# A state-space scan with a build-time planner: eight w buffers and four quads of rows, C products given to GpSimd by its lead, the shared weights prepared in the prologue

## The chip, the cores and the metric

The kernel runs on one core of one Trainium2 chip. The metric is the time of one execution on the device in microseconds (us). Three runs of the kernel before gave 6493.72, 6498.34 and 6510.17 us; the median is 6498.34 us. About 0.3% (20 us) is what such a measurement can tell apart.

In the text the engines have the names of the profile: PE is TensorE (matmuls), PEld its weight loads, DVE is VectorE, ACT is ScalarE, POOL is GpSimd, and SP is the engine whose queue issues all DMAs of this kernel.

## The reference, cut to what matters

Four images (batches) of 96 channels by 64 x 64 positions go through four layers, all in float32. Layer 0 is a two-dimensional selective scan. This is its core:

```python
xi = silu(depthwise_conv3x3(in_proj(layernorm(x))[:192]))        # 192 channels, 4096 positions
xs = [rows, columns, rows reversed, columns reversed]            # four directions k
dt = softplus(dt_proj(x_proj(xs)));  Bs, Cs = x_proj(xs)         # 16 states n
def step(hst, inp):
    dA = exp(dt_t[..., None] * A[None])
    dBx = dt_t[..., None] * B_t[:, :, None, :] * x_t[..., None]
    hst = hst * dA + dBx
    y_t = einsum('bkdn,bkn->bkd', hst, C_t)
```

Each of 192 channels has 16 states in 4 directions, and each state runs along 4096 positions. The sum over the states gives y. Then come a norm, a gate with silu(z), an output projection and a two-layer perceptron (the "tail" in the kernel). Layer 1 is a smaller scan (two directions, one state), layer 2 a Fourier transform over the positions with a perceptron in 8-bit floats, and layer 3 a linear attention with another such perceptron.

## The kernel before, in words

**The scan loop.** The scan of layer 0 is cut into 64 steps: four batches, four directions in the order 0, 1, 3, 2, four chunks of 1024 positions. A step has 24 units, numbered j (three groups of channels), q (four groups of states, the "quads") and p (two halves); a unit is a tile of 128 rows (32 channels by 4 states) by 1024 positions. There are 1536 units. For each of them

- `sources` (line 1517): POOL multiplies w = u * bb, where u is dt * x and bb holds the rows of B, broadcast by DMA;
- `decays` (1496): ACT computes h = exp(dt * A) into PSUM, which has two buffers for h, and copies the last state of the unit two before;
- `recurs` (1528): DVE scans h and w into h (TENSOR_TENSOR_SCAN), and then multiplies w = h * cc, the "C product", where cc holds the rows of C;
- `gathers` (1566): PE adds up the four states and the quads of w into the PSUM tile py, two units at a time, and then w is free.

The C product of some units is put aside: there the scan writes into w, and POOL multiplies w = w * cc (`side`, 1557). `aside` (1492) picks every 12th unit (11, 23, 35, ...), 127 in all.

**The buffers** are counted in line 1370: `WB, DB, RB, SIDE = 6, 3, 5, 12`. There are six w buffers: source i waits until the pair that holds unit i - 6 has been summed. There are three pairs of u and dt, and five each of bb and cc, one per quad of a step: the load for a quad waits until the quad five before it has been read for the last time (`loads_bc`, 1474). The u, dt, bb and cc tiles are 512 KB each as written on chip.

**The prelude of a step** (`preludes`, 1389) loads xi (four DMAs, `load_packed`), multiplies it by xw on PE, forms dt and dt * x (two POOL products of 128 x 1536 named dtu) and stores them to DRAM (dd, bc), from where the broadcast loads above read them.

**The background.** One thread, `others` (1647), does the rest while the loop runs, in series: `prepare` (folds weights of the tail and of layers 1 to 3 and stores them to DRAM as `prep_d`), then `front(b)` of batches 1 to 3 (norm, in-projection in four jobs two at a time, depthwise convolution, xi stored by rows and by columns), and then `rest(b)` of each batch: the tail with its four gates and eight groups, layer 1, and layers 2 and 3. The tail's chunks go in the order 3, 2, 1, 0, each when the loop has stored that chunk of y; the tail of a batch ends with BATCH_NORM_AGGREGATE. Batch 0's front runs alone ahead of the loop, in the prologue; after the loop what is left of batch 3 runs alone, with more banks and with DVE in POOL's place ("wide").

Each `front(b)` loads the in-projection's weights w_raw, multiplies them by the norm's bias and gain, centres them into w_in, and loads the convolution's diagonal weights dgs (two DMAs of 576 KB) right after.

**What sets the order.** No instruction is placed by hand. At build time a planner (class `Work`) keeps a clock for every engine, with a cost in us for every instruction (a POOL product of 1024 columns 2.36, a scan 2.34, a C product 1.23, a DMA 0.45 in SP's queue, then bytes/280e3 and 2.0 to land). Each thread says with `on(engine, events...)` what it waits for. The planner advances the thread that could start first (`choose`, 162; at equal times the lower rank), and the instructions are issued in that order on each engine. An engine works its own queue in order, so an instruction whose input is later than planned holds up all behind it. `wk_.me.end += t` tells the planner that what was just done takes t longer. The prologue ends for the planner when a condition holds (1663); only then are the pools for u, dt, bb, cc, w and Y opened, and the threads of the loop started.

All elementwise calls go through one helper, so nearly all DVE and POOL rows have line L254, ACT's L242 or L231, PE's L227, loads L275 and stores L279. The names of the tiles tell them apart.

Of the kernel before, what the change touches and what calls it, by code (L numbers as in the profile page):

```python
# [216 lines left out]
def tile_hybrid(ctx: ExitStack, tc: tile.TileContext, I: dict, out: bass.AP):  # L217
# [126 lines left out]
    l1A = const.tile([128, 2], F32, name="l1A")  # L344
    dsum = const.tile([128, 4], F32, name="dsum")
    centd = const.tile([C, C], F32, name="centd")
    diagD = const.tile([128, 3, 128], F32, name="diagD")

    xi_d = [dram.tile([2, NG, DI, HC], F32, name=f"xi_d{b}") for b in range(B)]
    z_d = [dram.tile([NG, DI, HC], F32, name=f"z_d{b}") for b in range(B)]  # L350
    y_d = [dram.tile([128, 3, 2048], F32, name=f"y_d{b}") for b in range(B)]
    x1_d = [dram.tile([C, L], F32, name=f"x1_d{b}") for b in range(B)]
    PREP = 1358
    prep = dram.tile([128, PREP], F32, name="prep_d")
    y1_d = [dram.tile([C, L], F32, name=f"y1_d{b}") for b in range(B)]
# [117 lines left out]
    def front(b):  # L473
        stx, (px_,) = pools(bg("fx"))
        xp01 = px_.tile([128, 66, 66], F32, name="xp01")
        xp2 = px_.tile([128, 34, 66], F32, name="xp2")
        dgs = [px_.tile([128, 9, 128], F32, name=f"dg{i}") for i in range(2)]
        ahead_ = b == 0
        if ahead_:
            stc, (xtp, ck) = pools(bg("f2"), bg("f2w"))  # L480
            xts = [xtp.tile([128, 64, rows], F32, name=f"xt{rows}") for rows in (64, 32)]
        st, (wp, wk) = pools(bg("f1"), bg("f1w"))
        w_raw = wp.tile([C, 384], F32, name="w_raw")
        w_in = wp.tile([C, 384], F32, name="w_in")
        yield on("sp")
        get(w_raw, I["w_inT"])
        yield on("pool")
        for xp, n in ((xp01, 66), (xp2, 34)):
            po_.memset(xp[:, :, 0:1], 0.0)
# [2 lines left out]
        po_.memset(xp01[:, 65, :], 0.0)  # L492
        po_.memset(xp2[0:64, 0, :], 0.0)
        po_.memset(xp2[64:128, 33, :], 0.0)
        (pb,) = yield on("pe", banks=1)
        for col, lo, m, r in ((0, 0, 128, 0), (1, 128, 64, 0), (1, 128, 64, 64), (2, 192, 128, 0), (3, 320, 64, 0), (3, 320, 64, 64)):
            mm(pb[r : r + m, col : col + 1], lhsT=w_raw[:, lo : lo + m], rhs=V("b1", C), start=True, stop=True)
        bias = wp.tile([128, 4], F32, name="bias")
        yield on("dve")
        ve.tensor_add(bias, pb[:, 0:4], V("bi", n=4))  # L500
        ve.tensor_scalar(w_raw, w_raw, V("g1", C), None, ALU.mult)
        drop(pb)
        yield from centred(w_in, w_raw, 384)
        xv = I["x"][b].rearrange("c (h g t) -> c g h t", h=2, t=HC)

        def inproj(gp):
# [63 lines left out]

            return job

        yield on("sp")
        for i in range(2):
            get(dgs[i], I[("dg01", "dg2")[i]])

        def conv(part, q):
            dg, xt, xp = dgs[part], xts[part], (xp01, xp2)[part]
# [38 lines left out]
        order = [(0, 0), (0, 1), (1, 0), (1, 1)] if ahead_ else []  # L617
        if ahead_:
            soon = wk_.add(par([conv(p, q) for p, q in order], 2))
        yield from par([inproj(gp) for gp in range(4)], 2, 4)  # L620
        if ahead_:
            yield on(None, lambda: soon.end if soon.done else None)
        st.close()
# [2 lines left out]

        if not ahead_:
            stc, (xtp, ck) = pools(bg("f2"), bg("f2w"))
            xts = [xtp.tile([128, 64, rows], F32, name=f"xt{rows}") for rows in (64, 32)]
        rest_ = [(p, q) for q in range(2, 4) for p in (1, 0)] if ahead_ else []  # L630
        rest_ += [(p, q) for p in (1, 0) for q in range(8 - 4 * p) if (p, q) not in order + rest_]
# [639 lines left out]

    def prepare():

        st, (wp,) = pools(bg("prep"))
        o = wp.tile([128, PREP], F32, name="prep")
        m1, tbias = o[0:C, 0:384], o[:, 384:387]
        dtc = o[0 : C + 1, 387:587].rearrange("p (k c) -> p k c", k=2)
# [6 lines left out]
        sc = wp.tile([C + 1, DI], F32, name="sc")  # L1284
        var, gam = (wp.tile([C, 1, C], F32, name=n) for n in ("var", "gam"))
        wq, sc1 = (wp.tile([C, C], F32, name=n) for n in ("wq", "sc1"))
        yield on("pool")
        po_.memset(o, 0.0)
        yield on("sp")
        get(m1, I["mlp1T"])  # L1290
# [25 lines left out]
        yield on("act")  # L1316
        copy(dtc[0:C, :, 0:C], pw[0:C, 0 : 2 * C].rearrange("p (k c) -> p k c", k=2))
        drop(pw)
        wk_.me.end += 15.0
        yield on("act", took=1.5, table=LN_EXP)  # L1320
        rstd(sc, bn[:, 3, :])
        rstd(var, var)
# [44 lines left out]
    ]  # L1367
    NS_ = len(steps)
    NU = UNITS * NS_
    WB, DB, RB, SIDE = 6, 3, 5, 12  # L1370
    made, weights, summed = {}, {}, {}
    anti = mybir.DependencyInfo(mybir.DependencyClass.Sync, mybir.DependencyReason.ANTI)
    live = dict(h={}, w={}, state={}, Y=None, py=None)
    fg = {}

    def place(i):
        n = i % UNITS
# [11 lines left out]
    def preludes():  # L1389
        ck, dp = fg["ck"], fg["dp"]  # L1390
        for g, (b, k, s, c) in enumerate(steps):
            need = [("front", b)] if k % 2 else rows_of(b, c)
            if g >= 3:
                need.append(("du", 6 * (g - 3) + 5))
            if g >= 1:
                need.append(("src", unit(g - 1, 0, 0, 0)))
            yield on("sp", *need)
            if s == 0:
                xw = ck.tile([128, 3, 128], F32, tag="xw", name="xw", bufs=1)
                get(xw, I["xw"][:, k])  # L1400
                dtw = ck.tile([64, 3, 128], F32, tag="dtw", name="dtw", bufs=1)
                get(dtw, I["dtw"][:, k])
                weights[b, k] = xw, dtw
            xw, dtw = weights[b, k]
            xi = ck.tile([128, 3, HC], F32, tag="xi", name="xi", bufs=1)
            load_packed(xi, xi_d[b][k % 2], c)
            d = made[g] = {}
            (px,) = yield on("pe", banks=1)
            for j in range(3):
                mm(px, lhsT=xw[:, j, :], rhs=xi[:, j, :], start=(j == 0), stop=(j == 2))  # L1410
            xd = ck.tile([128, HC], F32, tag="xd", name="xd", bufs=1)
            yield on("act")
            act(xd, px, AF.Identity, bias=V("ones"))
            drop(px)
            yield on("sp")
            bc = dp.tile([32, 2, HC], F32, tag="bc", name="bc")
            for hf in range(2):
                put(bc[:, hf], xd[64 + 32 * hf : 96 + 32 * hf])
            d["bc"] = bc.rearrange("n f t -> n (f t)")
            post("bc", g, stored=True)  # L1420
            dtu = ck.tile([128, 2, 3, HC], F32, tag="dtu", name="dtu", bufs=1)
            dd = d["dd"] = dp.tile([2, 3, 2, 32, 2, HC], F32, tag="dd", name="dd")
            for j0, j1 in ((0, 1), (1, 2), (2, 3)) if g == 0 else ((0, 3),):
                js = slice(j0, j1)
                for j in range(j0, j1):
                    (pd,) = yield on("pe", banks=1)
                    mm(pd, lhsT=dtw[:, j, :], rhs=xd[0:64], start=True, stop=True)
                    yield on("act", took=1.3)
                    act(dtu[:, 0, j], pd, AF.Abs)
                    act(dtu[:, 1, j], pd, AF.Relu)  # L1430
                    drop(pd)
                yield on("act", took=1.6, table=LN_EXP)
                act(dtu[:, 0, js], dtu[:, 0, js], AF.Exp, scale=-1.0)
                yield on("act", took=1.6, table=LN_EXP)
                act(dtu[:, 0, js], dtu[:, 0, js], AF.Ln, bias=one)
                if g == 0 and j1 == 3:
                    post("begun")
                yield on("pool")
                po_.tensor_add(dtu[:, 0, js], dtu[:, 0, js], dtu[:, 1, js])
                yield on("pool")  # L1440
                po_.tensor_mul(dtu[:, 1, js], dtu[:, 0, js], xi[:, js])
                yield on("sp")
                for p in range(2):
                    for hf in range(2):
                        r = p * 64 + hf * 32
                        put(
                            dd[:, js, p, :, hf, :].rearrange("t j d i -> d t j i"),
                            dtu[r : r + 32, :, js],
                        )
                for j in range(j0, j1):  # L1450
                    post("dd", g, j, stored=True)
            sync()
            post("dd", g)
# [35 lines left out]
                post(tag, n)  # L1489
                wk_.detach()  # L1490

    def aside(i):

        return i % SIDE == SIDE - 1 and i < NU - 1

    def decays():
        for i in range(NU + 2):
            if i >= 2:
                yield on("act", ("scan" if aside(i - 2) else "C", i - 2), *([("dt", 6 * place(i)[0] + 2 * place(i)[1] + place(i)[3])] if i < NU else []), took=1.3, table=LN_EXP, unit=min(i, NU - 1))
                g, j, q, p, n = place(i - 2)  # L1500
                b, k, s, c = steps[g]
                h = live["h"].pop(i - 2)
# [25 lines left out]
    def recurs():  # L1528
        for i in range(NU):
# [8 lines left out]
                live["state"][b, k] = fg["ck"].tile([128, 24], F32, tag="state", name="state")  # L1538
            h, w, state = live["h"][i], live["w"][i], live["state"][b, k]
            first = 0.0 if s == 0 else state[:, n : n + 1]  # L1540
            o = w if aside(i) else h
            if k >= 2:
                it = ve.tensor_tensor_scan(o[:, ::-1], h[:, ::-1], w[:, ::-1], first, ALU.mult, ALU.add)
            else:
# [3 lines left out]
                tc.add_manual_dep(it.ins, summed.pop(i - WB), anti, reason="sums of what lay in w")  # L1548
            if o is w:
                post("scan", i)  # L1550
                live["h"][i] = o
                continue
            yield on("dve")
            ve.tensor_mul(w, h, made[g]["cc", q])
            post("C", i)

    def side():

        for i in filter(aside, range(NU)):
            g, j, q, p, n = place(i)  # L1560
            yield on("pool", ("scan", i), *([("st", i)] if steps[g][2] < NCH - 1 else []))
            w = live["w"][i]
            po_.tensor_mul(w, w, made[g]["cc", q])
            post("C", i)

    def gathers():

# [78 lines left out]

    def others():
        yield on(None, ("front", 0))
        yield from prepare()
        for b in range(1, B):  # L1650
            yield from front(b)
        for b in range(B):
# [2 lines left out]
    with tc.manual_schedule():  # L1655
# [3 lines left out]
        st_ck, (ck, dp) = pools(sb("ck", 2), dict(name="sd", bufs=3, space=DRAM))  # L1659
        fg.update(ck=ck, dp=dp)  # L1660
        first = wk_.add(setup()), wk_.add(front(0))
        ts = [wk_.add(preludes(), 0)]
        wk_.run(
            lambda: first[0].done and ("inproj", 0) in wk_.events
            and not any(k.startswith("bs") for k in wk_.held.values())
        )
        mode["wide"] = False
# [193 lines left out]
```

## Time and profile before

| | us |
|---|---|
| median of three runs (6493.72 to 6510.17) | 6498.34 |
| the profiled execution | 6480.99 |
| its span, first to last instruction | 6479.2 |
| first scan of the loop starts | 92.1 |
| last C product of the loop ends | 5936.9 |
| DVE busy in the span | 5790.4 (89%) |
| PE busy | 5160.7 (80%) |
| POOL busy | 4737.6 (73%) |
| ACT busy | 4306.2 (66%) |

A group of the profile is a line, an engine, an operation and the tiles written and read, then the shape and the count; after the bar stand the busy time in us and the mean of one in ns, and after a second bar the idle time of the engine just before these instructions, with what ended most of it. In the windows view each engine has its busy us and, in brackets, its number of instructions. In the order of time a row starts with its start in us and its duration. This is the page's view of the span in 40 slices (a slice is 162 us), which shows how the loop fills DVE to slice 36 and how the rest follows:

```profile
DVE  6899999999989999999989999999989999997714
...
POOL 4778787887798787878798777787798778883000
```

The main marks of the background, from the order of time: fronts 1 to 3 begin at 277, 607 and 962 with the load of w_raw, and the third is done at 1311. The tail of batch 0 begins at 1313, those of batches 1 to 3 at 2805, 4277 and 5745, each behind the last output of the batch before (2799, 4271, 5738). Chunk 0 of y of batches 0 to 2 is stored at 1540, 3003 and 4476.

### The profile page before, as it was taken

Reading aid. Unit: us, or ns where it says so; the run is one execution under the profiler, and the core shown is the slowest. Engines: PE = TensorE matmul, PEld = TensorE weight load, DVE = VectorE, ACT = ScalarE, POOL = GpSimd, SP = SyncE. Lnnn points to the kernel's source line nnn. Section 1 sums busy time; section 2 is a strip of 40 time slices with the busy share of each in tenths; the row PEclk is TensorE's granted clock in tenths of the full one; section 3 lists DMA queues with packets and bytes.
Section 4 is the critical chain, followed back from the end, with each engine's and each line's share of the span. In section 5 each row is a group of like instructions: output and inputs, shape, how many; then the busy total and the mean of one; then the engine's idle time right before and its main releaser. Section 6 shows DMA issues by size and latency. Waiting matters only on the chain. (4 is left out here: it accounts for less than half of the span.)

```text
span 6479.2 us, 54904 instructions
## 1 busy us (share of the span) xinstructions
PE 5160.7 (80%) x15680; PEld 1622.7 (25%) x15680; DVE 5790.4 (89%) x3909; ACT 4306.2 (66%) x6506; POOL 4737.6 (73%) x2151
## 2 busy tenths in 40 slices
PE   8588887977867988767867988768868888777678
PEld 2122221222211332212211332212211332212264
DVE  6899999999989999999989999999989999997714
ACT  5465766666766558877766567877766557875635
POOL 4778787887798787878798777787798778883000
PEclk9789998988878999889979999888878999888788
DMA  5656556575565784665565785556565685552551
GB/s 170 198 186 200 172 172 192 173 221 178 161 199 173 231 274 152 187 190 181 169 197 163 226 272 172 171 184 184 179 186 166 219 283 182 166 176 82 158 153 46
DMA packets 532504, 1189.17 MB, mean 184 GB/s; under 512 B 90286, under 2 KB 163579, under 8 KB 532188
## 3 DMA queue, kind: packets, MB, share of 16 engines
q1 hardware_dynamic: 532200, 1185.66, 59.1%
q8 instruction: 124, 2.03, 0.1%
q14 instruction: 180, 1.47, 0.1%
HBM read 937.80 MB, written 247.63 MB: 183 GB/s over the span
## 5 line engine op out<-in xcount | busy, mean ns | idle before, releaser
L254 POOL TENSOR_TENSOR w<-u,bb 128x1024 f32<-128x1024 f32 x1536 | 3610.0, 2375 | 822.0 <-PE py L227 712.3
L254 DVE TENSOR_TENSOR_SCAN h<-h,state,w 128x1024 f32<-128x1024 f32 x1057 | 2483.1, 2349 | 178.5 <-ACT h L242 110.9
L227 PE MATMUL py<-w,sel 128*32 128x512 f32 x6144 | 1774.1, 937 | 424.4 <-DVE w L254 273.9
L242 ACT ACTIVATE h<-dt,negA 128x1024 f32<-128x1024 f32 x1536 | 1730.2, 1127 | 400.8 <-DVE w L254 311.0
L254 DVE TENSOR_TENSOR w<-h,cc 128x1024 f32<-128x1024 f32 x1409 | 1722.6, 1223 | 40.4
L254 DVE TENSOR_TENSOR_SCAN h<-h,w 128x1024 f32<-128x1024 f32 x352 | 805.5, 2288 | 77.6 <-ACT h L242 24.3
L231 ACT COPY state<-h 128x1 f32<-128x1 f32 x1056 | 166.0, 157 | 701.0 <-DVE w L254 699.6
L227 PEld LDWEIGHTS py<-w,sel 128*32 128x32 f32 x6144 | 182.2, 114 | 1438.6 <-DVE w L254 771.3
L254 POOL TENSOR_TENSOR w<-w,cc 128x1024 f32<-128x1024 f32 x127 | 299.1, 2355 | 114.4 <-ACT state L231 86.6
L227 PE MATMUL bm<-xp,dg 128*128 128x512 f32 x774 | 362.1, 610 | 0.0
L227 PE MATMUL bm<-xi,xw 128*128 128x512 f32 x378 | 224.6, 741 | 109.3 <-DMA xi<-xi_d 100.6
L254 POOL TENSOR_TENSOR dtu<-dtu 128x1536 f32<-128x1536 f32 (+1 forms) x66 | 221.7, 3359 | 102.3 <-ACT dtu L242 49.5
L242 ACT ACTIVATE dtu<-bm 128x512 f32<-128x512 f32 x382 | 210.0, 604 | 49.6 <-PE bm L227 48.3
L227 PE MATMUL bm<-xd,dtw 64*128 64x512 f32 x382 | 220.6, 658 | 22.8 <-ACT xd L242 9.1
L254 DVE TENSOR_TENSOR_SCAN w<-h,state,w 128x1024 f32<-128x1024 f32 x95 | 222.5, 2342 | 7.8 <-ACT h L242 4.0
L254 POOL TENSOR_TENSOR dtu<-dtu,xi 128x1536 f32<-128x1536 f32 (+1 forms) x66 | 221.2, 3352 | 4.2
L227 PEld LDWEIGHTS bm<-xp,dg 128*128 128x128 f32 x774 | 142.4, 192 | 281.3 <-issue 274.7
L227 PE MATMUL bm<-big,dg 96*96 96x512 f32 x450 | 206.0, 600 | 6.1 <-ACT state L231 4.8
L227 PE MATMUL py<-Y,eye 128*128 128x512 f32 x288 | 164.5, 654 | 53.5 <-ACT Y L231 44.3
L227 PE MATMUL bm<-x,cent 96*96 96x512 f32 x276 | 158.9, 672 | 42.8 <-POOL x L254 12.2
L242 ACT ACTIVATE bm<-bm,eps 96x512 f32<-96x512 f32 (+1 forms) x212 | 137.4, 648 | 80.1 <-PE bm L227 79.9
L242 ACT ACT_TABLE_LOAD x124 | 159.1, 1283 | 10.7 <-PE bm L227 6.9
(328 smaller groups left out, 6879.3 us busy)
## 6 DMA issues: line engine op xcount, KB each, us to landing
u<-dd SPq DMA_DIRECT2D x384, 512.0 KB
dt<-dd SPq DMA_DIRECT2D x384, 512.0 KB
bb<-bc SPq DMA_DIRECT2D x256, 512.0 KB
cc<-bc SPq DMA_DIRECT2D x256, 512.0 KB
dd<-dtu SPq DMA_DIRECT2D x252, 384.0 KB
xi<-xi_d SPq DMA_DIRECT2D x256, 192.0 KB
f_d<-fo SPq DMA_DIRECT2D x64, 384.0 KB
a<-f_d SPq DMA_DIRECT2D x64, 384.0 KB
```

Source lines behind the costliest of these rows:

```text
L227: return nc.tensor.matmul(o, lhsT=lhsT, rhs=rhs, **kw)
L231: return nc.scalar.copy(o, i, **kw)
L242: return nc.scalar.activation(o, i, func, **kw)
L254: return f(o, *a, **kw)
```

## The change

The diff, cut to its core:

```diff
+    bias = const.tile([128, 4], F32, name="bias")
+    w_d = dram.tile([C, 384], F32, name="w_d")
...
@@ front(b)
-        dgs = [px_.tile([128, 9, 128], F32, name=f"dg{i}") for i in range(2)]
         ahead_ = b == 0
         if ahead_:
+            dgs = [px_.tile([128, 9, 128], F32, name=f"dg{i}") for i in range(2)]
...
-        yield on("sp")
-        get(w_raw, I["w_inT"])
+        if not ahead_:
+            yield on("sp", ("w_in",))
+            get(w_in, w_d)
+        else:
+            w_raw = wp.tile([C, 384], F32, name="w_raw")
+            yield on("sp")
+            get(w_raw, I["w_inT"])
...
+        if ahead_:
             (pb,) = yield on("pe", banks=1)
...
             yield from centred(w_in, w_raw, 384)
+            def keep():
+                yield on("sp", ("xp", b, 3))
+                put(w_d, w_in)
+                post("w_in", stored=True)
+            wk_.add(keep())
...
-        yield from par([inproj(gp) for gp in range(4)], 2, 4)
+        yield from par([inproj(gp) for gp in range(4)], 3, 4)
...
         if not ahead_:
             stc, (xtp, ck) = pools(bg("f2"), bg("f2w"))
+            dgs = [xtp.tile([128, 9, 128], F32, name=f"dg{i}") for i in range(2)]
+            yield from taps_in()
@@ prepare()
-        st, (wp,) = pools(bg("prep"))
+        st, (wp,) = pools(sb("prep"))
...
-        yield on("pool")
+        yield on("pool", ("xp", 0, 0))
         po_.memset(o, 0.0)
...
-        wk_.me.end += 15.0
         yield on("act", took=1.5, table=LN_EXP)
@@ the loop
-    WB, DB, RB, SIDE = 6, 3, 5, 12
+    WB, DB, RB, APART, AHEAD = 8, 3, 4, 6, 4
+    sides = []
@@ preludes()
             load_packed(xi, xi_d[b][k % 2], c)
+            wk_.me.end += 2.0
@@ decays()
-                yield on("act", ("scan" if aside(i - 2) else "C", i - 2), ...
+                yield on("act", ("free", i - 2), ...
@@ recurs()
-            o = w if aside(i) else h
+            apart = i % 2 and (not sides or i - sides[-1] >= APART)
+            o = w if apart and i + AHEAD < NU and ("src", i + AHEAD) in wk_.events else h
...
             if o is w:
                 post("scan", i)
+                post("free", i)
                 live["h"][i] = o
+                sides.append(i)
                 continue
             yield on("dve")
             ve.tensor_mul(w, h, made[g]["cc", q])
             post("C", i)
+            post("free", i)
+        sides.append(None)
@@ others()
-        yield from prepare()
@@ the prologue
+        early_ = wk_.add(prepare(), 2)
         ts = [wk_.add(preludes(), 0)]
         wk_.run(
-            lambda: first[0].done and ("inproj", 0) in wk_.events
+            lambda: first[0].done and early_.done and ("inproj", 0) in wk_.events
```

What it does, part by part:

- **Which units are put aside.** The fixed list goes. When the planner reaches the scan of an odd unit i, it puts the unit aside if the last one put aside lies at least 6 units back and if the source product of unit i + 4 has already been planned. `side` follows that list as it grows: it waits for the scan, and, except in the last chunk of a direction, for ACT's copy of the state.
- **Buffers.** Eight w buffers for six, and four quads of bb and cc for five. In memory the two cancel out (two tiles of 4 KB a row each way).
- **The plan's count of an xi load** is 2.0 us longer, so that the xw matmuls are planned later.
- **prepare** leaves the background. It runs in the prologue as a thread of rank 2, from the first in-projected rows on, and the prologue isn't over for the planner before it is done. Its tiles lie where the loop's buffers are opened later. The 15 us that the plan added in its middle are gone.
- **The fronts of batches 1 to 3** load the finished w_in, which batch 0's front has stored, in place of making it again; the bias stays on chip. They load dgs only after the in-projection, into the space of the later pool, and do three in-projection jobs at a time.

The fetched weights, the products and the sums computed are the same as before.

More of the change, by code (lines that the diff above doesn't have):

```diff
@@ L482, in front @@
         st, (wp, wk) = pools(bg("f1"), bg("f1w"))
-        w_raw = wp.tile([C, 384], F32, name="w_raw")
         w_in = wp.tile([C, 384], F32, name="w_in")
-        yield on("sp")
-        get(w_raw, I["w_inT"])
+        if not ahead_:
[5 more added lines that the diff above has]
+            get(w_raw, I["w_inT"])
         yield on("pool")
@@ L494, in front @@
         po_.memset(xp2[64:128, 33, :], 0.0)
[L495 to L503, printed above, removed]
+        if ahead_:
+            (pb,) = yield on("pe", banks=1)
+            for col, lo, m, r in ((0, 0, 128, 0), (1, 128, 64, 0), (1, 128, 64, 64), (2, 192, 128, 0), (3, 320, 64, 0), (3, 320, 64, 64)):
+                mm(pb[r : r + m, col : col + 1], lhsT=w_raw[:, lo : lo + m], rhs=V("b1", C), start=True, stop=True)
+            yield on("dve")
+            ve.tensor_add(bias, pb[:, 0:4], V("bi", n=4))
+            ve.tensor_scalar(w_raw, w_raw, V("g1", C), None, ALU.mult)
+            drop(pb)
+            yield from centred(w_in, w_raw, 384)
+            def keep():
[3 more added lines that the diff above has]
+            wk_.add(keep())
         xv = I["x"][b].rearrange("c (h g t) -> c g h t", h=2, t=HC)
@@ L571, in inproj, with taps_in @@
             return job
-        yield on("sp")
-        for i in range(2):
-            get(dgs[i], I[("dg01", "dg2")[i]])
+        def taps_in():
+            yield on("sp")
+            for i in range(2):
+                get(dgs[i], I[("dg01", "dg2")[i]])
+        if ahead_:
+            yield from taps_in()
         def conv(part, q):
@@ L628, in front @@
             stc, (xtp, ck) = pools(bg("f2"), bg("f2w"))
+            dgs = [xtp.tile([128, 9, 128], F32, name=f"dg{i}") for i in range(2)]
+            yield from taps_in()
             xts = [xtp.tile([128, 64, rows], F32, name=f"xt{rows}") for rows in (64, 32)]
@@ L1490, in loads_bc @@
                 wk_.detach()
-    def aside(i):
-        return i % SIDE == SIDE - 1 and i < NU - 1
     def decays():
@@ L1498, in decays @@
             if i >= 2:
-                yield on("act", ("scan" if aside(i - 2) else "C", i - 2), *([("dt", 6 * place(i)[0] + 2 * place(i)[1] + place(i)[3])] if i < NU else []), took=1.3, table=LN_EXP, unit=min(i, NU - 1))
+                yield on("act", ("free", i - 2), *([("dt", 6 * place(i)[0] + 2 * place(i)[1] + place(i)[3])] if i < NU else []), took=1.3, table=LN_EXP, unit=min(i, NU - 1))
                 g, j, q, p, n = place(i - 2)
@@ L1555, in recurs, with chosen @@
             post("C", i)
+            post("free", i)
+        sides.append(None)
     def side():
-        for i in filter(aside, range(NU)):
-            g, j, q, p, n = place(i)
-            yield on("pool", ("scan", i), *([("st", i)] if steps[g][2] < NCH - 1 else []))
+        n = 0
+        while True:
+            def chosen():
+                if len(sides) <= n or sides[n] is None:
+                    return 0.0 if len(sides) > n else None
+                i = sides[n]
+                if steps[place(i)[0]][2] < NCH - 1:
+                    return wk_.events.get(("st", i))
+                return wk_.events["scan", i]
+            yield on("pool", chosen)
+            i = sides[n]
+            if i is None:
+                return
+            g, j, q, p, _ = place(i)
             w = live["w"][i]
@@ L1564, in side @@
             post("C", i)
+            n += 1
     def gathers():
```

## The prediction

> **What bounds the kernel now.** I read the page first, for each engine's share and for where it changes. The scan over the 1536 units of layer 0 runs on VectorE from 92.1 us to 5936.9 us, which is 90% of the span, so the answer is sought in that stretch.
>
> ```profile
> 92.00:5936.00 5844.00, 4679.95 (x14018) 1372.72 (x14019) 5526.38 (x3462) 3981.48 (x5938) 4725.64 (x2127) 0.89 0.62 191
> ```
> This is the windows view of the stretch: length, then PE, PEld, DVE, ACT and POOL busy. DVE is busy 5526 of 5844 us, which leaves 318 idle; POOL has 1118 idle. The groups view says what fills both engines.
>
> ```profile
> L254 DVE TENSOR_TENSOR w<-h,cc 128x1024 f32<-128x1024 f32 x1409 | 1722.6, 1223 | 40.4
> L254 POOL TENSOR_TENSOR w<-w,cc 128x1024 f32<-128x1024 f32 x127 | 299.1, 2355 | 114.4 <-ACT state L231 86.6
> L254 POOL TENSOR_TENSOR w<-u,bb 128x1024 f32<-128x1024 f32 x1536 | 3610.0, 2375 | 822.0 <-PE py L227 712.3
> ```
> A C product costs DVE 1223 ns, or POOL 2355 ns plus 0.90 us of wait (114.4/127). POOL's largest idle time is 712 us of waiting until PE has summed an old w. Then the waits, of DVE over the loop and of PE from 250 to 5880 us (us in total, times, longest):
>
> ```profile
> DVE h L254 <- ACT h L242: 135.3, 126, 8.3
> DVE h L254 <- ACT state L231: 57.7, 43, 8.5
> DVE h L254 <- POOL w L254: 40.1, 37, 2.6
> ```
> ```profile
> PE bm L227 <- DMA xi<-xi_d: 93.7, 31, 8.5
> ```
> DVE seldom waits for POOL. So DVE's own work sets the loop. But there is a second chain that nearly sets it too: the background thread, which does fronts 1 to 3 and then, batch by batch, tail, layer 1, 2 and 3. The order of time (start, length), SP's queue around 5738 us and then DVE at the end of batch 3's tail:
>
> ```profile
> 5671.50 0.53 SPq L279 DMA_DIRECT2D y_d<-Y  x1
> ...
> 5738.15 0.32 SPq L279 DMA_DIRECT2D out<-x  x1
> ...
> 5744.93 0.54 SPq L275 DMA_DIRECT2D rt<-in_r_tail  x1
> ```
> ```profile
> 5991.09 0.37 DVE L254 BATCH_NORM_AGGREGATE mv<-stat 96x2 f32<-96x48 f32 x1
> ```
> Chunk 3 of batch 3 was stored at 5672, but its tail began only at 5745, when batch 2's last output had gone out at 5738. The four tails end (BATCH_NORM_AGGREGATE) at 1639, 3104, 4576 and 5991: rounds of 1465 and 1472 us, against 1461 us for a batch of the loop. The two are almost equal, and a shorter loop is only worth what the background follows.
>
> **The change, part by part.**
> *More C products on POOL.* Now every 12th unit is aside (127). After it, an odd unit is aside if 6 or more have passed and POOL's source product is planned 4 units ahead. At most 1536/6, less the end, is 255. By the order of time, POOL had begun 4 units ahead at 114 of 768 odd units and 2 or more ahead at 585 (76%); with two more w buffers, a lead that the buffers cap moves up by up to two. A step's dtu products (2 x 3.4 us) and each extra aside eat that lead. Bounds: 0 and 128 extra; I take 103 (230 in all, the nearest to 76% with some delay): 103 x 1.223 = 126 us off DVE. POOL can hold it: busy 4726, waits other than for PE 406, plus 103 x 3.26 = 335, makes 5467 of some 5740.
> A table in the Trainium skill (GPSIMD Engine Reference, 4.1 Engine selection) speaks against this: two-input elementwise work belongs on VectorE, GpSimd being about twice as slow. The rows agree (2355 against 1223, 1.93 times). By that rule the products would stay and the 126 us would be nothing; the engine with 1118 us idle decides for the move.
> *POOL later for DVE.* DVE's waits for POOL are 43.8 us with 127 asides, 0.34 each: 103 x 0.34 = 36 us back. Bounds: minus 44 (eight buffers remove them all) and 103 x 2.355 = 243 (each aside holds up the next scan in full).
> *Four quads for five.* A bb or cc load may start one quad later. Between the end of the last reader and the first use, with four, today's times leave 19.7 us (median; least 14.3) for bb and 22 to 25 for cc (least 18.7). In the prologue a u load took 4.3 us from issue to use. Bounds: 0, and 63 steps x 2.2 us (73/34, a wait for u) = 136 on POOL. I take 5, since no wait for bb or cc shows in the loop's long waits.
> *Weights in the prologue.* prepare's DVE operations at 218 to 265 us sum to 12.9 us (four take about 2.3 us each), and the fronts' two on w_raw and bias to 4.5: 17 us leave the loop. Its 15 loads and the store move ahead of the first dd, u and dt loads in SP's queue; SP is idle from 12 to 44 us, then mostly waits for conv outputs, and prepare waits for the first in-projection (about 42). Some 3.5 us of DVE work falls among the depthwise taps that lead to the first scan. The loop opens only when prepare is done, and its first buffers take prepare's space. Bounds for the first scan: minus 2 and plus 20 (a chain from 42 with its 679 KB store ending at 100 instead of 80). I take plus 5. Against that, DVE's third early stall (8.3 us at 233, ACT waiting 9.8 us for a dt load queued behind those 15 loads) shrinks: minus 5.
> A rule of the Trainium skill (SBUF — State Buffer, Who interferes with whom) says that a VectorE instruction with two SBUF inputs waits for a GpSimd one that reads SBUF. The trace agrees: prepare's 96x1 products take 2274 ns beside POOL and 156 without. The C products read h from PSUM and show no such thing (1156 to 1266 ns), so more of POOL costs them nothing.
> *xi counted 2 us longer.* It moves the xw matmuls behind other PE work. Up to the 94 us of PE idle, none of it DVE's; bounds for the time 0 and minus 25 a round. *Three in-projections at once, dgs loaded late:* only in the fronts, which end at 1313 where y of batch 0 ends at 1540: 0, at worst 10 us on a front and hidden.
> Loop: -126 - 17 + 36 + 5 + 5 - 5 = **-102**, so VectorE's last product at about 5835.
>
> **What the background lets through.** Tail 0 waits for y at 1540, a quarter along, so it ends 26 us earlier. In the next two rounds chunk 1's groups end 11 us before chunk 0's gate product (3030 to 3041, 4503 to 4514): 11 us spare in each, so the last output of batch 2 comes 26 + 11 + 11 = 48 us earlier, at 5690. Tail 3 starts at 5697; its four pairs of groups took 91 and 62 us in the loop and 43 to 45 after it: 5792, 5850, 5895, 5939, against 5991. That is 52 us. PE stalls for xi returned to the background give some 6 us in each of three rounds: **70 us** in all, less than the loop's 102. From 5991 to the end (488 us) nothing changes. Own time 6481 (span 6479.2 and 1.8 around it) - 70 = 6411. The median of the runs, 6498.34, lies 17 above that execution: I predict 6428.
>
> **Rivals.** *The whole loop gain arrives* (18%): the background's steps also wait for DVE and get faster as DVE empties. For: DVE is 93% busy while layer 1 runs beside the loop (1367 of 1470 us in three windows). Against: two rounds of nearly equal length. 6498 - 102 = 6396; with all 128 asides and no added wait near 6350.
> *Nothing much* (13%): asides are hardly chosen, or POOL's lateness returns the 126 us (103 x 1.2 us a piece). 6478 to 6518.
> *Slower* (12%): the background becomes longer, through POOL. A batch's background has 84 products on POOL (64 of layer 1, 16 sums, 4 gates) in about three parallel jobs, 28 in series. Each that meets an added aside waits up to 3.26 us: 91 us a round, 274 in all, +200. It decides from 0.83 us a product (70/3/28). Against: added asides occupy 335/5740 = 6% of POOL, on average 0.1 us. For: in-order queues cluster. A midway 1.35 us a product: +44, 6542.
> My forecast has 57% (6405 to 6478). Three runs can hardly tell less than 0.3%, about 20 us, from no change: faster 0.57 + 0.18, same 0.13, slower 0.12. The range 6365 to 6500 holds the forecast, most of the first rival and about half of the second: 0.8.
>
> **What would show it.** About 230 POOL rows w<-w,cc and 1306 DVE rows w<-h,cc; POOL's wait for PE below 400 us; DVE's last product near 5835; prepare's rows before 92 and the first scan at 92 to 102; batch 2's last output near 5690, and tail 3 still starting right behind it. Rounds under 1450 would speak for the first rival, over 1475 for the last. Under 170 asides, or DVE waits for POOL above 150 us, and the step on asides is wrong. Waits for bb or cc would show that four quads are too few.

## The result, and the profile after

The changed kernel took 6386.00 us (median of five runs, 6379.59 to 6390.87) against 6498.34 (five runs, 6481.92 to 6510.17): a ratio of 0.9826, interval 0.9807 to 0.9846, or 112 us less. The profiled execution took 6390.87 us where that of before took 6480.99: 90 us less. The two differ because the profile of before lies 17 us below its median and that of after 5 us above; steps are compared between the two profiles, verdicts between the medians.

The windows view of the loop, from the first scan at 98.4 us to the last C product, which ends at 5848.8 (length, then PE, PEld, DVE, ACT and POOL busy):

```profile
98.00:5849.00 5751.00, 4669.05 (x13943) 1378.91 (x13945) 5442.87 (x3380) 3983.83 (x5935) 4873.00 (x2188) 0.88 0.61 194
```

The loop is 94 us shorter (5750 against 5845), and begins 6 us later. DVE is busy 84 us less and idle 308 us, 10 us less than before; POOL is busy 147 us more. The groups:

```profile
L254 DVE TENSOR_TENSOR w<-h,cc 128x1024 f32<-128x1024 f32 x1345 | 1644.6, 1223 | 48.1 <-DMA cc<-bc 9.4
...
L254 POOL TENSOR_TENSOR w<-w,cc 128x1024 f32<-128x1024 f32 x191 | 450.6, 2359 | 144.4 <-ACT state L231 96.9
...
L254 POOL TENSOR_TENSOR w<-u,bb 128x1024 f32<-128x1024 f32 x1536 | 3607.5, 2377 | 615.1 <-PE py L227 419.3
```

191 units went aside, not the 230 that I expected: 64 C products left DVE, 78 us. POOL's wait for PE fell from 712 to 419 us. The two more w buffers alone don't do this: the run fixed12 below has them, with the old 127 asides, and there the wait is 677 us. Most of the fall comes with the added asides, which fill POOL's idle time:

```profile
L254 POOL TENSOR_TENSOR w<-u,bb 128x1024 f32<-128x1024 f32 x1536 | 3605.4, 2377 | 809.1 <-PE py L227 677.4
```

What DVE waits for in the loop of the changed kernel, in the waits view (us in total, times, longest):

```profile
DVE h L254 <- ACT h L242: 164.7, 155, 10.4
DVE h L254 <- ACT state L231: 36.9, 31, 4.4
DVE h L254 <- POOL w L254: 23.9, 17, 5.3
```

The wait for POOL became less (24 against 40 us), the wait for ACT's h became more (165 against 135). The end of the background, from the order of time on SP's queue and then on DVE:

```profile
5590.23 0.54 SPq L279 DMA_DIRECT2D y_d<-Y  x1
...
5666.39 0.40 SPq L279 DMA_DIRECT2D out<-x  x1
...
5675.12 0.54 SPq L275 DMA_DIRECT2D rt<-in_r_tail  x1
```
```profile
5847.59 1.21 DVE L254 TENSOR_TENSOR w<-h,cc 128x1024 f32<-128x1024 f32 x1
...
5901.94 0.37 DVE L254 BATCH_NORM_AGGREGATE mv<-stat 96x2 f32<-96x48 f32 x1
```

Batch 2's last output comes 72 us earlier (5666), and the last tail ends 53 us after the last C product; before, 54 us after. So the end moved with the loop, all of it: 88 us at the loop's end, 89 at the tail's, 90 in the span.

### The profile page after: what moved, and what is told of

The parts are those of the page before. It is cut to its first block, busy times and chain, and to the rows that moved or that the text cites. A ratio compares the mean times of both kernels' runs of the same rounds, so it can differ in the third digit from the quotient of the medians.

```text
span 6389.1 us, 54746 instructions
## 1 busy us (share of the span) xinstructions
PE 5157.9 (81%) x15634; PEld 1634.6 (26%) x15634; DVE 5711.2 (89%) x3841; ACT 4319.8 (68%) x6521; POOL 4888.8 (77%) x2215
## 5 line engine op out<-in xcount | busy, mean ns | idle before, releaser
L254 DVE TENSOR_TENSOR_SCAN h<-h,state,w 128x1024 f32<-128x1024 f32 x1005 | 2360.9, 2349 | 162.0 <-ACT h L242 116.2
L227 PE MATMUL py<-w,sel 128*32 128x512 f32 x6144 | 1742.2, 939 | 447.2 <-DVE w L254 311.1
L242 ACT ACTIVATE h<-dt,negA 128x1024 f32<-128x1024 f32 x1536 | 1728.6, 1126 | 390.4 <-DVE w L254 321.0
L254 DVE TENSOR_TENSOR w<-h,cc 128x1024 f32<-128x1024 f32 x1345 | 1644.6, 1223 | 48.1 <-DMA cc<-bc 9.4
L254 DVE TENSOR_TENSOR_SCAN h<-h,w 128x1024 f32<-128x1024 f32 x340 | 777.9, 2288 | 79.4 <-ACT h L242 48.5
L254 POOL TENSOR_TENSOR w<-w,cc 128x1024 f32<-128x1024 f32 x191 | 450.6, 2359 | 144.4 <-ACT state L231 96.9
L227 PE MATMUL bm<-xp,dg 128*128 128x512 f32 x792 | 378.4, 620 | 10.2 <-DMA dg<-in_dg 10.1
L254 DVE TENSOR_TENSOR_SCAN w<-h,state,w 128x1024 f32<-128x1024 f32 x147 | 344.2, 2342 | 11.1 <-ACT h L242 7.6
L227 PE MATMUL bm<-xi,xw 128*128 128x512 f32 x384 | 213.9, 701 | 38.7 <-DMA xi<-xi_d 35.3
L227 PE MATMUL bm<-big,dg 96*96 96x512 f32 x450 | 221.4, 634 | 11.6 <-ACT u L242 6.3
```

What stands on the lines that cost most here:

```text
L227: return nc.tensor.matmul(o, lhsT=lhsT, rhs=rhs, **kw)
L242: return nc.scalar.activation(o, i, func, **kw)
L254: return f(o, *a, **kw)
```

## The experiments

Theory 1 says that the loop on DVE sets the time and what is behind it follows. Theory 2, which my prediction rested on, says that the background is as long as the loop and holds back part of any gain. Theory 3 says that the buffers, the weights and the count of xi do most of it, and the asides little. "Loop" and "idle" below are the loop's length and DVE's idle time in it, from the order of time of each profile. Ratios are to the kernel before.

| kernel | asides | us (median) | ratio (interval) | loop | idle |
|---|---|---|---|---|---|
| before | 127 | 6498 | 1 | 5845 | 318 |
| changed | 191 | 6386 | 0.9826 (0.9807 to 0.9846) | 5750 | 308 |
| fixed12 | 127 | 6438 | 0.9914 (0.9892 to 0.9937) | 5798 | 273 |
| none_aside | 0 | 6491 | 0.9995 (0.9985 to 1.0004) | 5865 | 213 |
| all_odd6 | 256 | 6464 | 0.9953 (0.9937 to 0.9968) | 5775 | 418 |
| ahead3 | 216 | 6453 | 0.9933 (0.9915 to 0.9952) | 5741 | 328 |
| tail_late | 190 | 6427 | 0.9896 (0.9879 to 0.9913) | 5751 | 313 |
| old_buffers | 5 | 6515 | 1.0018 (1.0007 to 1.0028) | 5871 | 228 |
| prep_back | 181 | 6434 | 0.9899 (0.9883 to 0.9916) | 5798 | 355 |
| no_xi | 192 | 6385 | 0.9821 (0.9799 to 0.9844) | 5749 | 323 |
| old_fronts | 188 | 6382 | 0.9825 (0.9802 to 0.9848) | 5734 | 308 |
| only_buffers | 127 | 6520 | 1.0031 (1.0020 to 1.0042) | 5898 | 360 |
| rb4 | 127 | 6514 | 1.0031 (1.0019 to 1.0042) | 5878 | 365 |
| only_prep | 127 | 6512 | 1.0021 (1.0008 to 1.0034) | 5874 | 356 |

**How many asides: the fixed list, none, every sixth unit.** Three edits of one line in `recurs`:

```diff
-            o = w if apart and i + AHEAD < NU and ("src", i + AHEAD) in wk_.events else h
+            o = w if i % 12 == 11 and i < NU - 1 else h       # fixed12
+            o = h                                             # none_aside
+            o = w if apart and i < NU - 1 else h              # all_odd6
```

> The changed kernel with the old fixed list of asides (units 11, 23, 35, ...: 127 in place of 191). Theory 1, the loop rules: 64 C products of 1.22 us come back to DVE, 78 us, so about 6464 us, and the last C product of the loop near 5925. Theory 2, the background holds part of the gain: what the loop loses was partly never had, so the time rises by less than the loop, by 20 to 50 us (6406 to 6436), the loop still by about 78. Theory 3, the gain comes mostly from the buffers, the weights and the xi count: the time stays within 20 us of 6386.

> The changed kernel with no unit aside: all 1536 C products on DVE. Theory 1: 191 x 1.223 = 234 us on top of 6386, about 6620, one for one. Theory 2: less than one for one near the changed kernel, then one for one: 6560 to 6600. If POOL's lateness costs DVE time (my 0.34 us for each aside), 191 x 0.34 = 65 us of it come back: about 6555.

> The changed kernel without the test of POOL's lead: every sixth unit aside, 256 in place of 191. Theory 1 with POOL still able: 65 x 1.223 = 80 us less, about 6306. Theory 2: the loop gets shorter, the time by 30 or less, 6355 to 6386. If POOL is late when its lead is not asked for, DVE waits for w grow from 24 us to over 100, and the time is 6370 to 6450.

With the fixed list the time was 6438, 52 us more; the loop got 47 us longer, not 78, so on average each of the 64 asides was worth 0.7 us of the loop and 0.8 us of the time in place of 1.22. It is an average and no more: the 64 lie in all four batches (10, 19, 16 and 19 of them), but against fixed12 the changed loop is shorter only in batches 2 and 3 (by 25 and 30 us) and 3 and 5 us longer in batches 0 and 1. The other 60 of the 112 us don't come from the choice of asides, so Theory 3 has about half. With none it was 6491, 105 us more for 191 asides: 0.55 each. DVE's idle time tells where the rest went. It rises with the asides: 213 us with none, 273 with 127 (0.48 for each), 308 with 191 (0.54 for each of the 64 more), 418 with 256 (1.70 for each of the last 65, which no lead was asked for). These are not waits for POOL in the first place. I sorted the idle time in front of every scan by how many units before it the last aside lay. In the changed kernel a scan right behind an aside waits 0.46 us on average (72 of 191 wait more than 0.3), all other scans 0.11. Of the 89 us that DVE waits right behind asides, 68 end with ACT's h and 18 with ACT's copy of the state. Behind an aside DVE goes from scan to scan, without the 1.22 us of a C product between, and ACT has that much less time for the next h. The wait for h in none_aside, and the waits for ACT and for POOL in all_odd6, fit this:

```profile
DVE h L254 <- ACT h L242: 77.4, 84, 8.7
```
```profile
DVE h L254 <- ACT h L242: 198.4, 166, 12.2
DVE h L254 <- POOL w L254: 68.5, 35, 7.0
```

There is a second loss, in DVE's busy time, but no price per aside can be read from it. DVE's busy time in the loop less the durations of its scans and C products is 189 us in none_aside, 218 in fixed12, 215 in the changed kernel and 209 in all_odd6. Most of the difference lies in four groups of small operations (gm, rl, kvacc times its mask, hs of the first piece), a few instructions in each batch: 24 us in none_aside, 45 in fixed12, 41 in the changed kernel, but 33 in all_odd6, with the most asides, and 30 in the kernel before. How long one of them takes goes by what POOL does at that moment; the last section shows one.

**A lead of three.** `AHEAD` 3 in place of 4:

```diff
-    WB, DB, RB, APART, AHEAD = 8, 3, 4, 6, 4
+    WB, DB, RB, APART, AHEAD = 8, 3, 4, 6, 3
```

> The changed kernel with a lead of three units asked for in place of four: some 20 to 40 more asides. At the mean price measured so far (1.22 us saved, 0.54 lost as DVE idle, some 0.2 in small DVE operations) they give 10 to 20 us: 6365 to 6380. At the price of the asides that no lead was asked for (1.7 us lost each): 6390 to 6420.

6453, which both prices miss. The loop was as expected, 25 asides more and its last C product at 5841.5, 7 us earlier than in the changed kernel. But the time was 67 us longer, so the loop doesn't set it here. SP's queue and DVE show what does:

```profile
5782.80 0.32 SPq L279 DMA_DIRECT2D out<-x  x1
...
5785.71 0.54 SPq L275 DMA_DIRECT2D rt<-in_r_tail  x1
```
```profile
5840.25 1.23 DVE L254 TENSOR_TENSOR w<-h,cc 128x1024 f32<-128x1024 f32 x1
...
5956.03 0.37 DVE L254 BATCH_NORM_AGGREGATE mv<-stat 96x2 f32<-96x48 f32 x1
```

Batch 2's last output is 116 us later than in the changed kernel. The tail of batch 3 starts only 56 us before the loop ends, and it ends 115 us after it, not 53. From the end of one tail to the last output of the batch, the background took 1214 and 1238 us in batches 1 and 2, against 1126 and 1154 in the changed kernel. all_odd6 is the same case (1224 and 1222; the span ends 589 us after the loop in place of 540). A background that becomes longer is what my last rival foresaw. In none_aside it took 1183 us in both batches and in fixed12 1159 and 1165, so its length doesn't simply grow with the asides; what lengthens it in these two kernels isn't shown.

**Is the background the bound in the changed kernel?** In tail_late the tails of batches 1 and 2 wait for one more chunk of y:

```diff
     def rest(b):
+        if b in (1, 2):
+            yield on(None, ("y", b, 1))
         st, (pp,) = pools(bg("post"))
```

> The changed kernel, but the tails of batches 1 and 2 begin only when chunk 1 of y is stored (2892 and 4326 us in the changed kernel's profile, in place of 2796 and 4209). Theory 2, the background is as long as the loop and has some 11 us spare a round: the delay of about 100 us is passed on, batch 2's last output comes 70 to 110 us later and the time rises by 50 to 90 us (6436 to 6476). Theory 1, the background has slack that only hides behind the wait for chunk 0: the time stays within 20 us of 6386.

6427, 41 us more, between the two. The loop did not change by a microsecond (5751). Only the first of the two waits held anything up: the tail of batch 1 began 84 us later, at 2879, while that of batch 2 began at 4349, behind the last output of batch 1 and after its chunk 1. The delay was passed on: the last output of batch 2 came 93 us later, and the tail ended 94 us after the last C product:

```profile
5759.68 0.32 SPq L279 DMA_DIRECT2D out<-x  x1
```
```profile
5848.63 1.23 DVE L254 TENSOR_TENSOR w<-h,cc 128x1024 f32<-128x1024 f32 x1
...
5943.35 0.37 DVE L254 BATCH_NORM_AGGREGATE mv<-stat 96x2 f32<-96x48 f32 x1
```

So of 93 us that the background came later the end felt 41; the other 52 were no loss. Not all of them need be waiting time that the changed kernel had to spare: batch 3's tail, from its load of rt to its end, takes 227 us in the changed kernel and 182 in tail_late, where more of it runs after the loop. The fourteen kernels fall into two groups: where batch 2's last output lies 182 us or more before the last C product, the span ends 536 to 548 us after that product, whatever the kernel; where it lies 91, 90 or 59 us before it (all_odd6, tail_late, ahead3), the span ends 589, 581 and 606 us after it. No kernel lies between 91 and 182, so where the one passes into the other is open: near 130 if each microsecond below it costs one, but the three points fit a half for each from 182 on as well. Theory 1 holds for the change as made, with 182, as to what sets the end; theory 2 takes over somewhere in the next 90 us.

**The buffers.** Six w buffers and five quads in the changed kernel; then eight and four, and four quads alone, in the kernel before:

```diff
-    WB, DB, RB, APART, AHEAD = 8, 3, 4, 6, 4
+    WB, DB, RB, APART, AHEAD = 6, 3, 5, 6, 4        # old_buffers
...
-    WB, DB, RB, SIDE = 6, 3, 5, 12
+    WB, DB, RB, SIDE = 8, 3, 4, 12                  # only_buffers
+    WB, DB, RB, SIDE = 6, 3, 4, 12                  # rb4
```

> The changed kernel with six w buffers and five quads. With a lead that never went above 4 in the kernel before, the test of 4 units is met at a sixth of the odd units, so I expect 60 to 110 asides, more waits of POOL for PE (over 550 us) and DVE idle near 300 us. If the buffers are what cuts DVE's idle time, 6450 to 6490; if only the number of asides counts at 0.8 us each, 80 asides against 191 make 6475; if neither does, within 20 of 6386.

> The kernel before with eight w buffers and four quads, and nothing else. The fixed-list run, with all parts of the change but the choice of asides, was 59 us faster than the kernel before, 44 of it DVE idle time in the loop. If the buffers did that: 6440 to 6465. If the weights, the fronts and the xi count did it: 6480 to 6505, and POOL's wait for PE falls without DVE getting anything. If four quads cost more than eight w buffers give: above 6505.

> The kernel before with four quads, six w buffers. The two buffer changes together cost the kernel before 20 us. If the fourth quad is the price: about 6520 or more, with waits for bb, cc. If it is the eight w buffers, which shift the order of the plan: within 10 of 6500.

With six buffers the planner found 5 units to put aside, not 60 to 110: in the plan a lead of four units hardly ever comes about (on the chip POOL had begun four units ahead at 206 of the 768 odd units). The time, 6515, is 24 us above that of none_aside, with an idle time near it (228 against 213). POOL then waits 1011 us for PE:

```profile
L254 POOL TENSOR_TENSOR w<-u,bb 128x1024 f32<-128x1024 f32 x1536 | 3598.0, 2366 | 1207.5 <-PE py L227 1011.2 <-DMA u<-dd 153.6 <-DVE w L254 17.4
```

In the kernel before, eight buffers with four quads cost 20 us and four quads alone 20 us: they are no gain in themselves, but the choice by lead needs them. Eight w buffers with five quads would leave 17.5 KB a row where Y takes 24, so the fifth quad is their price. rb4 shows no wait for bb or cc among its long ones, so late rows of B or C don't explain the 20 us. It has other stalls, the two longest of 18.5 and 16.5 us from scan to scan at 1014 and 1379 us, where the kernel before has none. Which order of the plan makes them I haven't traced.

**The weights.** prepare back in the background in the changed kernel, and in the prologue in the kernel before. This is the core of the diff; its memory, the start of its first memset and the 15 us of the plan go with it:

```diff
@@ prep_back: the changed kernel; only_prep: the reverse in the kernel before
     def others():
         yield on(None, ("front", 0))
+        yield from prepare()
...
-        early_ = wk_.add(prepare(), 2)
```

> The changed kernel with the shared weights prepared in the background again, behind front 0, as before the change. My sum gave this part 17 us of DVE's loop less 5 for the prologue. If that holds, 6392 to 6410, the first scan back at 92 us, and the step from 108 back in the loop's first three steps. The fixed-list run lost only 3 us of DVE busy time against the kernel before where I had counted 17; if the other small DVE operations had simply become longer beside a busier POOL, that stays so here and the time is 6395 to 6410; if the part is worth nothing it stays within 10 of 6386.

> The kernel before with the shared weights prepared in the prologue, and nothing else. Undoing this part in the changed kernel cost 48 us, most of it in the loop's first two steps. If it is a gain of its own (prepare and its 15 loads no longer stand between the loop's first dt and u loads): 6440 to 6465. If it is only a gain beside the other parts (front 1, three jobs at once, right behind): 6480 to 6505.

Back in the background it cost 48 us, four times my 12. The loop's first two steps took 115 and 105 us in place of 92 and 94, 34 us, and the largest piece is one stall. ACT, in prep_back's order of time:

```profile
206.18 1.12 ACT L242 ACTIVATE h<-dt,negA 128x1024 f32<-128x1024 f32 x1 [20.72 <-DMA dt<-dd]
```

SP's queue says why: 18 stores of front 0 are issued from 181.6 to 199.6 us and the next step's first u and dt loads behind them.

```profile
181.61 17.98 SPq L279 DMA_DIRECT2D xi_d<-xt  x18
199.63 0.63 SPq L275 DMA_DIRECT2D u<-dd  x1
200.31 0.60 SPq L275 DMA_DIRECT2D dt<-dd  x1
```

In the changed kernel three pairs of u and dt loads (178.6 to 186.7) go ahead of those 18 stores. So this stall is made by an order of the plan and not by prepare's own loads, which are issued only from 208.7 us; why the plan took that order isn't shown. And alone, in the kernel before, the move gained nothing: its first two steps were about 23 us shorter (91 and 89 against 95 and 109), but later stalls of 17.5 and 17.6 us at 904 and 1269 took it back, 14 us slower in all.

**xi and the fronts.** The changed kernel without the 2 us, and with the old `front(b)`:

```diff
             load_packed(xi, xi_d[b][k % 2], c)
-            wk_.me.end += 2.0                        # no_xi
...
-            get(w_in, w_d)                           # old_fronts
+        get(w_raw, I["w_inT"])
...
-        yield from par([inproj(gp) for gp in range(4)], 3, 4)
+        yield from par([inproj(gp) for gp in range(4)], 2, 4)
```

> The changed kernel without the 2 us that the plan adds to a load of xi. If the xi count only takes PE's idle time away, PE waits some 100 us for xi again and the time stays within 10 of 6386. If those stalls reach DVE through the state copies and the h tiles (ACT held up behind xd), DVE idle rises by 20 to 40 us: 6405 to 6425.

> The changed kernel with the fronts as they were (w_in made anew, dgs loaded early, two in-projection jobs at once). My sum gave this part 4.5 us. If that is its size: within 15 of 6386. The parts found so far leave some 30 us open (fixed list -59, of which the weights -48 and the buffers +20): if the fronts are those, 6405 to 6425.

Neither makes a difference (6385 and 6382 against 6386). PE's wait for xi, 100.6 us before and 35.3 in the changed kernel, is 76.5 without the 2 us, and the time is the same: these 41 us of PE's stall don't reach it.

## Why the prediction was right or wrong, point by point

The direction was right, and 6386 lies in the range 6365 to 6500, but not within my forecast's own stretch (6405 to 6478). It lies 10 us below the 6396 of the rival which I gave 18%, the whole loop gain arriving. That rival's reason, a background that gets faster, is seen in part: from the end of a tail to the last output it took 1126 and 1154 us in batches 1 and 2, in place of 1167 and 1163. That DVE is the cause isn't shown.

- **"A shorter loop is only worth what the background follows", 52 us of 102.** This step failed. I took the four pairs of groups of the last tail at 91, 62, 45 and 44 us as the tail's own pace. The last was not: it waits for chunk 0 of y, which the end of the loop gives. Counted from the load of rt, the pairs took 96, 62, 43 and 45 us before and 90, 62, 43 and 31 in the changed kernel, and the tail ends 53 us after the loop, where it was 54; in all eleven kernels whose batch 2 is done 182 us or more before the loop's end, it is 51 to 57. In tail_late only 41 of 93 us of delay reached the end, where I had every one count. My sum of the pairs also dropped 4 us (5792 with 62, 45 and 44 makes 5943, not 5939). The tail's end came 89 us earlier and not 70; 15 of these 19 us are the shorter tail (227 us from the load of rt, where I had 242), the other 4 its earlier start.
- **The rounds.** Batch 2's last output at 5666 (I said 5690, or 5672 with the 18 us that I added for PE's stalls) was near, but by luck. I had the tails of batches 0 to 2 end 26, 37 and 48 us earlier; they ended 37, 24 and 63 earlier. The rounds took 1478 and 1432 us, one beyond my sign for the last rival and one beyond that for the first, and the 18 us can't be PE's stalls for xi, since without the 2 us the output comes at 5656.
- **The extra asides, 103 at 1.22 us.** 64. By the order of time POOL had begun four units ahead at 617 of 768 odd units in none_aside, more than the 585 that I got by shifting the old leads by two, but only at 510 in the changed kernel: I had named the lead that the asides themselves eat and given it too little. Size wrong, mechanism right.
- **What asides give back, 0.34 us each, through waits for POOL.** The runs say 0.48 to 0.54 of idle time, and the largest part of it comes through ACT's h behind the asides; waits for POOL fell from 40 to 24 us. The row that I took was the wrong one, so that the size was near is luck.
- **17 us of small DVE work out of the loop.** prepare's and the fronts' operations left, but DVE's busy time besides scans and C products fell only from 221 to 215 us: the four groups of small operations named above took 41 us where they had taken 30, longer beside POOL. The Trainium skill's rule that I quoted (SBUF — State Buffer, Who interferes with whom) was right about which, and I drew from it only that the C products are safe.
- **The first scan 5 us later:** 6.3 (98.4 against 92.1). **The early stalls 5 us less:** the first two steps took 186 us against 203, 17 less.
- **Four quads, 5 us; xi, 6 us a round; the fronts, nothing.** POOL waited 64 us for bb in the changed kernel and DVE 9 for cc, which I had called the sign that four quads are too few. xi is worth nothing measurable, and so are the fronts.
- **The offset.** I put the profile of before 17 us below its median and carried that over. The profile of after lies 5 us above its median; 22 us of the 42 between 6428 and 6386 come from that.

Loop: forecast -102, measured -88 at its end. That it is so near is chance: 48 us of missing asides, 11 us of small operations and 1 us at the start are missing, and DVE's idle time, which I had rise by 36 us, fell by 10.

What stays open: the parts don't add up. Everything but the choice of asides (fixed12) gave 59 us, yet the buffers alone cost 20, the weights alone cost 14, and xi and the fronts were worth nothing in the changed kernel. Some of it must lie in how the parts meet in the plan. The traces narrow it down. Between the profiles fixed12's loop is 47 us shorter than that before, and 42 of these lie in batch 0, beside which prepare and the fronts ran (1400 us against 1442): DVE is busy 18 us less there, which is the size of my 17 for prepare and the fronts, and idle 23 us less. The seven kernels that have the new buffers, the weights in the prologue and asides take 1396 to 1409 us for batch 0. With only one of the first two it is 1450 (only_buffers), 1456 (only_prep) and 1435 (prep_back). That points to buffers and weights together, but no run has just these two edits, and single stalls of 15 to 25 us come and go with the order of the plan.

## What to carry to other kernels

Work moved from a full engine to one with idle time is worth its duration less what its absence exposes: here 1.22 us became 0.55 to 0.8 on average, for the larger part since the next instruction's other input had less time to be made. When two chains of nearly equal length end together, look at what the last piece waits for before taking its length as its pace. And where a planner makes the order, parts tested alone can cost what they gain together: test them by taking them out of the whole as well.

## What the runs showed of the hardware

A DVE instruction with two SBUF inputs can be held up for several POOL instructions in a row, not one. In fixed12, from the order of time on DVE and on POOL:

```profile
2081.82 9.80 DVE L254 SCALAR_TENSOR_TENSOR hs<-rl,hs 128x192 f32<-128x192 f32 x1
```
```profile
2079.75 11.66 POOL L254 TENSOR_TENSOR w<-u,bb 128x1024 f32<-128x1024 f32 x5
```

In none_aside the same instruction fell into a pause of POOL, which waited 3.75 us for PE until 2125.4:

```profile
2124.86 0.34 DVE L254 SCALAR_TENSOR_TENSOR hs<-rl,hs 128x192 f32<-128x192 f32 x1
```

0.34 us against 9.80: DVE's instruction ended 0.2 us after the last of five products that followed each other without a gap. In the changed kernel kvacc<-kvacc,rbk (8.81 us at 2643, beside the last four of five products in a row) and hs (9.69 us at 2100, beside four) show the same: each ended 0.1 to 0.2 us after POOL's run of products. It isn't always so: kvacc<-kvacc,rbk of fixed12 at 2625 (0.76 us) ended 0.1 us after the first of several products that followed each other without a gap. Which of the two happens the traces don't say. In all fourteen kernels the instructions of the four groups that took over 1.2 us in the loop, 129 of them, ended at most 0.25 us after a POOL instruction, and 24 of them had waited for two or more. The C products, with h in PSUM, don't wait so: 1223 ns on average in both kernels.
